# The last column phase of a two-layer scan network: its first finished quarter is handled in two halves of 16 columns

## The chip, the cores and the metric

One core of one Trainium2 chip runs the whole program in one launch. The metric is the device time of an execution, in microseconds (us). The kernel before takes 4107.3 us (median of 3 runs, 4107.22 to 4108.03). One more execution was taken by the profiler; it took 4108.49 us, and every row of the profile is from that one. Engines: PE is TensorE (PEld its weight loads), DVE VectorE, ACT ScalarE, POOL GpSimd, SP SyncE; a row that ends in "q" (SPq, ACTq) is the engine's part in issuing transfers.

## The reference

The input x has 32 images, 48 channels, 64 rows and 128 columns, in float32. Two layers follow one another. Each normalises its input in 16 groups of channels, runs four scans one after the other over the normalised planes, and adds its own input back at the end. The scans go down the rows, up the rows, right over the columns and left over the columns. One step of a scan adds to a line a one-dimensional convolution (48 to 48 channels, 5 taps) of the line before:

```python
def step(w, b):
    def f(carry, inp):
        nxt = inp + _conv1d(carry, w, b)
        return (nxt, nxt)
    return f
```

Each step needs the result of the step before, so a scan over 128 columns is a chain of 127 steps. The left scan begins at the last column and ends at column 0. A column of the result is known as soon as the left scan has passed it; the layer's input at that column is then added (the residual), and the sum is written out in the layout of x.

## The kernel before

The program goes through 12 phases, each a down and up scan over rows or a right and left scan over columns, for a part of the images. The change is in the last one, number 11: the column scans of layer 1 for the second pair of image groups.

**How a column phase is laid out.** The 128 columns are four quarters of 32, quarter 0 at the left edge and quarter 3 at the right. A quarter is six units (`UNITS`, L804: three blocks of channels and lines by two halves of the images); a unit is 128 partitions by 2048 floats, 1 MB. A phase has only three slots of SBUF for its four quarters, so quarter 3 shares a slot with quarter 0: when the right scan has passed quarter 0, `spill_unit` (L823) writes that one to DRAM, `load_unit` (L809) brings quarter 3, and in the left scan, once quarter 3 is finished, `spill_unit` brings quarter 0 back. The scan steps are written in `step` (L902): nine matrix products on PE and three additions on DVE (L929).

**How a quarter is finished.** `load_residual` (L832) brings the layer's input of a unit from the DRAM tensors named `mid` into one of six tiles: four of `arena` and two spare ones, whose rows read `early` (the second spare lies over the weights of the right scan). When the left scan has passed the quarter, `add_residual` (L847, one instruction at L850 on POOL) adds the tile into the unit; `permute_unit` (L865, L872) copies the unit into the tile in the order of the output, 8 copies shared by POOL and ACT; `store_result` (L880) writes the tile to `out` by three or four transfers on the queues of SP and ACT. A store runs along 32 columns, so its packets are 128 B each, 8192 to a unit. Quarter 3 is finished first, then 2, 1 and 0. The last one, quarter 0, is finished after the scan by `last_results` (L1195), where DVE adds and DVE, POOL and ACT copy.

**What else is around.** The phase before leaves some of its results in a DRAM buffer, `held`. During phase 11 SP sends them from there to `out` (`let_result`, L893; rows `out<-held`).

**What sets the order.** `plan_cols` (L1116) writes an agenda: `at(t, fn, ...)` puts a piece of work at a time t that is counted in scan steps, and the program is emitted in that order. `left` is the step at which the left scan begins and `first` of a quarter is `left + 34 + 32 * n_done`, with 4.5 steps between units. Each engine then works through its own list in order, as soon as what a row waits for is there, whatever its time in the agenda. Transfers of the queues of SP and ACT are given eight completion semaphores (`DMAHW0` to `DMAHW7` in the rows below), one after the other, in the order of the builder's schedule and whichever queue they are in; a transfer is issued only when the one that had its semaphore before has landed. One copy on ACT of a single column (L307, `early<-arena 128x1`) reads a column that the left scan writes, at `left + 10`; in the kernel before it stands ahead of the six residual loads of quarter 3, which `plan_cols` puts at `left + 16`, and holds them until that column is there.

Of the kernel before, what the change touches and what calls it, by code (L numbers as in the profile page):

```python
# [31 lines left out]
ALU = mybir.AluOpType  # L32
# [10 lines left out]
E8 = 8  # L43
# [34 lines left out]
def weight_runs():  # L78
# [24 lines left out]
PHASES = (  # L103
    ("rows", 0, 0),
    ("rows", 0, 1),
    ("rows", 0, 2),
    ("rows", 0, 3),
    ("cols", 0, 0),
    ("cols", 0, 1),
    ("rows", 1, 0),  # L110
    ("rows", 1, 1),
# [10 lines left out]
def kernel(  # L122
# [8 lines left out]
    nc = tc.nc  # L131
    B, _, H, W = x.shape
    NK = W // E8
    NH = H // E8
    KQ = NK // NQ
    WQ = W // NQ
    N = NK * GB
    RUN = KQ * GB
# [158 lines left out]
    def dma(dst, src, queue=None):  # L297
        (queue or nc.sync).dma_start(dst, src)
# [21 lines left out]
    def pieces(o):  # L320
        return [(e, c0, c1, p0) for e, c0, c1, g, p0 in PIECES if g == o]
# [3 lines left out]
    def slots(k):  # L325

        return (0, 1, 2) if k % 2 == 0 else (2, 1, 0)
# [476 lines left out]
    UNITS = [(g, half) for g in range(NG) for half in range(2)]  # L804

    def quarter(k, j):
        return slot[slots(k)[j % 3]].rearrange("p (o s n) -> p s o n", s=2, o=NG)
# [50 lines left out]
    def by_image(t):  # L858

        return t.rearrange("p (a e k b) -> p a b k e", a=NH, e=E8, b=GB)  # L860
# [13 lines left out]
    def in_output(j, g, e):  # L874


        t = out[g * GB : (g + 1) * GB].rearrange("b c (a e) w -> e (c a) b w", e=E8)
        return t[e, :, :, j * WQ : (j + 1) * WQ]

    def store_result(k, j, i, perm):  # L880
        pair = PHASES[k][2]
        o, half = UNITS[i]
        for n, (e, c0, c1, p0) in enumerate(pieces(o)):
# [2 lines left out]
            queue = nc.scalar if n % 2 and k == len(PHASES) - 1 else nc.sync  # L886
            dma(dst.rearrange("(c a) b n -> c a b n", a=NH), src, queue)

    def hold_result(j, i, perm):
        o, half = UNITS[i]  # L890
        dma(held[j, half][o], perm, nc.scalar)
# [145 lines left out]
    def at(t, fn, *args):  # L1037
        agenda.append((t, len(agenda), fn, args))

    def spread(t, gen, every):  # L1040


        def go(t):
            if next(gen, "end") != "end":
                at(t + every, go, t + every)
                agenda.sort(key=lambda a: a[:2])

        at(t, go, t)
# [67 lines left out]
    def plan_cols(k, t0, prev):  # L1116
        _, layer, pair = PHASES[k]
        n = 2 * NG
        after = prev == "cols"
        for i in range(n):  # L1120
            early = 30 if after else 58 if k - 1 in JOINED else 54
            at(t0 - early + 2 * i, load_unit, k, 0, i)
            at(t0 + (3 if after else -24 + 2 * i), load_unit, k, 1, i)
            at(t0 + (38 if after else 8) + 2 * i, load_unit, k, 2, i)
            at(t0 + 33 + 2 * i, spill_unit, k, i, False)
            at(t0 + 50 + 2 * i, load_unit, k, 3, i)
        final = k == len(PHASES) - 1
        left = t0 + W - 1
        end = left + W - 1
        for i in range(n):  # L1130

            t = left + 64 + 2 * i if layer == 0 else left + 39.5 + 4.5 * i
            at(t, spill_unit, k, i, True)
        units = []
        for n_done, j in enumerate((3, 2, 1, 0)):
            first, every = left + 34 + 32 * n_done, 4.5
            if j == 0 and PHASES[k + 1 if not final else k][0] == "rows":
                first, every = (end + 29, 6) if pair else (first, 7)
            units += [(first + every * i, j, i) for i in range(n)]
        stats = None  # L1140
        if layer == 0:
            stats = ResultStatsV(f"r{2 * pair}"), ResultStatsA(f"r{2 * pair + 1}")
        tiles = [stage[:, i] for i in range(4)]
        if layer:
            tiles += spare_tiles[0 : 2 if final else 1]
        n = len(tiles)
        direct = [u for u in units if not (final and u[1] == 0)]

        for u, (t, j, i) in enumerate(direct):
            nat = tiles[u % n]  # L1150
            o, half = UNITS[i]
            if u < n:
                at(left + 16, load_residual, k, j, i, nat)
            if layer == 0:
                if u >= n:
                    at(max(direct[u - n][0] + 3, t - 21), load_residual, k, j, i, nat)
                at(t, add_residual, k, j, i, nat)
                at(t + 4, keep_result, k, j, i)
                unit = quarter(k, j)[:, half, o]
                if half == 0:  # L1160
                    for b in range(GB):
                        at(t + 5 + b, stats[0].take, j, o, unit, b)
                else:
                    at(t + 1, stats[1].take, j, o, unit)
            else:

                at(t, add_residual, k, j, i, nat)
                at(t + 2.5, permute_unit, k, j, i, nat, (nc.gpsimd, nc.scalar, nc.scalar))
                if final or j not in HELD:
                    at(t + 4.5, store_result, k, j, i, nat)  # L1170
                else:
                    at(t + 4.5, hold_result, j, i, nat)
                if final and j == 1:
                    at(t + 4.7, load_residual, k, 0, i, last_tiles(k)[i])

                if u >= 2 and u - 2 + n < len(direct):
                    at(t + 4.6, load_residual, k, *direct[u - 2 + n][1:], tiles[(u - 2) % n])
        if layer == 0:
            spread(units[-1][0] + 14, pair_scaling(pair, stats, 8), 1)
        if layer:  # L1180

            at(left + 10, nc.scalar.copy, junk[:, BN - 1 :], quarter(k, 3)[:, 0, 0, RUN - 1 : RUN])
        if layer and not final:
            todo = [(j, half, e) for j in HELD for half in range(2) for e in range(E8)]
            for n, what in enumerate(todo):
                at(end + 63 + 1.9 * n, let_result, *what)
        if final:
            at(end + 4, last_results, k)

    def last_tiles(k):  # L1190

        s = slot[slots(k)[2]].rearrange("p (i n) -> p i n", i=2 * NG)
        return [s[:, i] for i in range(2 * NG)]
# [11 lines left out]
    for k, (kind, *_) in enumerate(PHASES):  # L1205
        n = (H if kind == "rows" else W) - 1
        starts.append(end - 2 * n if k in JOINED else end)
        end = starts[-1] + (2 if k in JOINED else 1) * n + (2 if k + 1 in JOINED else 1) * n
    for k, (kind, layer, _) in enumerate(PHASES):
        (plan_rows if kind == "rows" else plan_cols)(k, starts[k], PHASES[k - 1][0])  # L1210
# [279 lines left out]
```

## Time and profile before

| | before |
|---|---|
| median of 3 runs | 4107.3 us |
| profiled execution | 4108.49 us |
| its span on the core | 4106.8 us |
| PE busy, of the span | 4012.3 us, 98% |
| DVE busy | 2078.8 us, 51% |
| ACT busy | 1306.9 us, 32% |
| POOL busy | 789.0 us, 19% |
| packets of transfers, all | 2253898, of them under 512 B 2008848 |

The span is what the engines and queues record; 1.7 us of the profiled execution lie around it. In the page's 40 slices each digit is a slice of 102.7 us, so the whole left scan of the last phase is in the last three, and slices are too coarse for it: the table by stretches and the lists of transfers with their times are what to read there.

### The profile page before, as it was taken

How to read it: one execution, taken by the hardware profiler on the slowest of the kernel's cores; microseconds unless marked ns; L12 is line 12 of the kernel's file. 1: busy time of each engine (PE TensorE's matmuls, PEld its weight loads, DVE VectorE, ACT ScalarE, POOL GpSimd, SP SyncE). 2: the span in 40 equal slices, each digit the busy share in tenths (PEclk: the TensorE clock that was granted, in tenths of full speed). 3: DMA queues.
4: the chain of work that ended last, by engine and by line, in shares of the span. 5: the costliest groups of instructions: out<-in, count | busy, mean ns of one | idle time of the engine just before them, and what ended most of it. 6: DMA issues, size and time to landing. Idle time of an engine off the chain costs nothing. (4 is left out here: it accounts for less than half of the span.)

```text
span 4106.8 us, 85201 instructions
## 1 busy us (share of the span) xinstructions
PE 4012.3 (98%) x34360; PEld 3927.0 (96%) x34360; DVE 2078.8 (51%) x6137; ACT 1306.9 (32%) x2628; POOL 789.0 (19%) x672
## 2 busy tenths in 40 slices
PE   6999999999999999999999999999999999999994
PEld 5999999999999999999999998888999999999994
DVE  6454454544444567546655443333444444444444
ACT  4557466430000355003773633434000002300122
POOL 5631303100000243002411000000000025610353
PEclk9999999999999999999999999999999999999997
DMA  9898897967993499804996965666698039999799
GB/s 299 220 223 185 245 189 218 171 108 97 147 181 60 141 245 288 193 2 155 242 161 143 142 102 96 101 108 104 103 166 202 1 77 245 299 251 155 147 234 196
DMA packets 2253898, 681.57 MB, mean 166 GB/s; under 512 B 2008848, under 2 KB 2206656, under 8 KB 2231232
## 3 DMA queue, kind: packets, MB, share of 16 engines
q1 hardware_dynamic: 2117568, 595.36, 70.3%
q10 hardware_dynamic: 135936, 80.77, 8.2%
q8 instruction: 270, 4.42, 0.5%
q14 instruction: 124, 1.02, 0.1%
HBM read 399.11 MB, written 295.93 MB: 169 GB/s over the span
## 5 line engine op out<-in xcount | busy, mean ns | idle before, releaser
L850 POOL TENSOR_TENSOR arena<-arena 128x2048 f32<-128x2048 f32 x80 | 362.5, 4547 | 1714.3 <-PE step_00l L915 521.3
L790 ACT ACTIVATE arena<-arena,offsetr,scaler 128x128 f32<-128x128 f32 (+1 forms) x576 | 345.2, 688 | 348.8 <-DMA arena<-mid 322.5
L648 ACT ACTIVATE early<-arena 128x256 f32<-128x256 f32 x192 | 129.7, 676 | 837.0 <-POOL arena L850 830.6
L790 ACT ACTIVATE arena<-arena,offset,scale 128x256 f32<-128x256 f32 (+2 forms) x360 | 249.0, 787 | 91.8 <-DMA arena<-xin 81.6
L709 POOL COPY arena<-arena 128x256 f32<-128x256 f32 x340 | 201.0, 653 | 383.7 <-DMA arena<-in_x 230.2
L915 PE MATMUL step_01r<-arena,early 128*128 128x128 f32 x2286 | 249.8, 272 | 0.0
L915 PE MATMUL step_11r<-arena,early 128*128 128x128 f32 x2286 | 249.2, 272 | 0.0
L915 PEld LDWEIGHTS step_11r<-arena,early 128*128 128x128 f32 x2286 | 248.7, 184 | 0.4 <-DVE arena L929 0.3
L915 PEld LDWEIGHTS step_01r<-arena,early 128*128 128x128 f32 x2286 | 248.9, 184 | 0.2
L915 PE MATMUL step_00r<-arena,early 128*128 128x128 f32 x2286 | 248.8, 272 | 0.0
L915 PEld LDWEIGHTS step_00r<-arena,early 128*128 128x128 f32 x2286 | 248.5, 184 | 0.2 <-DVE arena L929 0.2
L915 PE MATMUL step_10l<-arena,wleft 128*128 128x128 f32 x2286 | 248.5, 272 | 0.0
L915 PE MATMUL step_11l<-arena,wleft 128*128 128x128 f32 x2286 | 248.5, 272 | 0.0
L915 PE MATMUL step_00l<-arena,wleft 128*128 128x128 f32 x2286 | 248.4, 272 | 0.0
L915 PE MATMUL step_01l<-arena,wleft 128*128 128x128 f32 x2286 | 248.4, 272 | 0.0
L915 PE MATMUL step_10r<-arena,early 128*128 128x128 f32 x2286 | 248.4, 272 | 0.0
L915 PEld LDWEIGHTS step_10l<-arena,wleft 128*128 128x128 f32 x2286 | 248.4, 184 | 0.0
L915 PEld LDWEIGHTS step_11l<-arena,wleft 128*128 128x128 f32 x2286 | 248.4, 184 | 0.0
L915 PEld LDWEIGHTS step_00l<-arena,wleft 128*128 128x128 f32 x2286 | 248.4, 184 | 0.0
L915 PEld LDWEIGHTS step_01l<-arena,wleft 128*128 128x128 f32 x2286 | 248.4, 184 | 0.0
L915 PEld LDWEIGHTS step_10r<-arena,early 128*128 128x128 f32 x2286 | 248.4, 184 | 0.0
L872 ACT COPY arena<-arena 128x256 f32<-128x256 f32 x172 | 99.6, 656 | 366.6 <-POOL arena L850 234.7
(545 smaller groups left out, 6870.1 us busy)
## 6 DMA issues: line engine op xcount, KB each, us to landing
xin<-arena SPq DMA_DIRECT2D x94, 512.0 KB, 4.5
arena<-in_x SPq DMA_DIRECT2D x18, 2048.0 KB, 10.5
upa<-arena SPq DMA_DIRECT2D x192, 192.0 KB, 3.8
arena<-upa SPq DMA_DIRECT2D x96, 384.0 KB, 9.9
arena<-xin SPq DMA_DIRECT2D x96, 384.0 KB, 10.6
upb<-arena SPq DMA_DIRECT2D x192, 192.0 KB, 3.9
arena<-upb SPq DMA_DIRECT2D x96, 384.0 KB, 10.9
arena<-xin SPq DMA_DIRECT2D x174, 192.0 KB, 4.2
```

Of the source, the lines that this page charges most:

```text
L648: nc.scalar.activation(junk[:, 0:n], view[:, b], AF.Identity, accum_out=self.sum[:, i, j : j + 1])
L709: copy(dst[:, r, q], src[:, r0 + r, q])
L790: nc.scalar.activation(args[0], args[0], AF.Identity, bias=args[2], scale=args[1])
L850: eng.tensor_tensor(unit, unit, nat, ALU.add)
L872: copy(by_w(perm)[:, a], src[:, a])
L915: nc.tensor.matmul(part(turn(whole(ps[o]))[0:m], -s), weights[:, i, at : at + m], part(turn(src(i)), s), start=seen[o] == 1, stop=seen[o] ...
```

## The change

Quarter 3 of the last phase, the one that is finished first, is handled in two halves of 16 columns: the right half (columns 112 to 127) from 17 steps after the left scan's begin, the left half (96 to 111) at the place where the whole unit was handled. For each half POOL adds the half unit into the residual tile (L900 of the new kernel; the sum stands in the tile, where it stood in the unit before), POOL and ACT copy it back into the unit in the order of the output (L906), and the store takes it from the unit. A store of a half runs along 16 columns, 64 B to a packet, so a half has as many packets as a whole unit had. The six residual loads of quarter 3 are put at `left - 14` to `left - 6` (five) and `left + 2` (the one whose tile lies over the weights), and the six of quarter 2 all follow their unit's stores.

```diff
--- before.py
+++ after.py
@@ -886,6 +886,33 @@
             queue = nc.scalar if n % 2 and k == len(PHASES) - 1 else nc.sync
             dma(dst.rearrange("(c a) b n -> c a b n", a=NH), src, queue)
 
+    def part_of_unit(t, half):
+
+        n = RUN // 2
+        return t.rearrange("p (m h n) -> p h m n", h=2, n=n)[:, half]
+
+    def finish_part(k, j, i, nat, half, store):
+
+        o, g = UNITS[i]
+        unit = quarter(k, j)[:, g, o]
+        here, sums = part_of_unit(unit, half), part_of_unit(nat, half)
+        if not store:
+            nc.gpsimd.tensor_tensor(sums, here, sums, ALU.add)
+            src = by_image(nat)[:, :, :, 2 * half : 2 * half + 2]
+            dst = here.rearrange("p (a b) (k e) -> p a b k e", a=NH, e=E8)
+            for a in range(NH):
+                eng = (nc.gpsimd, nc.scalar, nc.scalar)[a % 3]
+                copy = eng.copy if eng is nc.scalar else eng.tensor_copy
+                copy(dst[:, a], src[:, a])
+            return
+        pair = PHASES[k][2]
+        w0 = half * WQ // 2
+        for n, (e, c0, c1, p0) in enumerate(pieces(o)):
+            dst = in_output(j, 2 * pair + g, e)[c0 * NH : c1 * NH, :, w0 : w0 + WQ // 2]
+            queue = nc.scalar if n % 2 else nc.sync
+            src = here[p0 : p0 + c1 - c0].rearrange("p (a b) n -> p a b n", a=NH)
+            dma(dst.rearrange("(c a) b n -> c a b n", a=NH), src, queue)
+
     def hold_result(j, i, perm):
         o, half = UNITS[i]
         dma(held[j, half][o], perm, nc.scalar)
@@ -1149,6 +1176,13 @@
         for u, (t, j, i) in enumerate(direct):
             nat = tiles[u % n]
             o, half = UNITS[i]
+            if u < n and final:
+                at(left - 14 + 2 * i if i < n - 1 else left + 2, load_residual, k, j, i, nat)
+                for part, first in ((1, left + 17 + 2.5 * i), (0, t - 1)):
+                    at(first, finish_part, k, j, i, nat, part, False)
+                    at(first + 3, finish_part, k, j, i, nat, part, True)
+                at(t + 3, load_residual, k, *direct[u + n][1:], nat)
+                continue
             if u < n:
                 at(left + 16, load_residual, k, j, i, nat)
             if layer == 0:
@@ -1173,7 +1207,7 @@
                 if final and j == 1:
                     at(t + 4.7, load_residual, k, 0, i, last_tiles(k)[i])
 
-                if u >= 2 and u - 2 + n < len(direct):
+                if u >= (n + 2 if final else 2) and u - 2 + n < len(direct):
                     at(t + 4.6, load_residual, k, *direct[u - 2 + n][1:], tiles[(u - 2) % n])
         if layer == 0:
             spread(units[-1][0] + 14, pair_scaling(pair, stats, 8), 1)
```

The order of instructions moves in three places. The first is ACT's list at the end of phase 10's results (`held_111<-arena`) and the begin of the last left scan. `mid_86` and `mid_87` are the residuals of quarter 3; the last two rows of the loads (`early<-mid_87`) are the tile over the weights. Before:

```order
L298 DMA held_111<-arena 128x2048 [waits DMAHW3_49,Activation_49,Pool_49]
L307 COPY early<-arena 128x1 [waits DMAHW5_49,DMAHW6_49,DMAHW4_49,DVE_49]
L298 DMA arena<-mid_86 128x8x256 [waits DMAHW4_49,DMAHW0_49]
L298 DMA arena<-mid_87 128x8x256 [waits DMAHW5_49]
L298 DMA arena<-mid_86 128x8x256 [waits DMAHW6_49,DMAHW1_49]
L298 DMA arena<-mid_87 128x8x256 [waits DMAHW7_49,DMAHW3_49]
L298 DMA early<-mid_86 96x8x256 [waits DMAHW0_49]
L298 DMA early<-mid_86 32x8x256 [waits DMAHW1_49]
L298 DMA early<-mid_87 96x8x256 [waits DMAHW2_49,PE_49]
L298 DMA early<-mid_87 32x8x256 [waits DMAHW3_49]
```

And now:

```order
L298 DMA held_111<-arena 128x2048 [waits DMAHW3_49,Activation_49,Pool_49]
L298 DMA arena<-mid_86 128x8x256 [waits DMAHW5_49,DMAHW0_49]
L298 DMA arena<-mid_87 128x8x256 [waits DMAHW7_49,DMAHW6_49]
L298 DMA arena<-mid_86 128x8x256 [waits DMAHW1_49]
L298 DMA arena<-mid_87 128x8x256 [waits DMAHW3_49]
L298 DMA early<-mid_86 96x8x256 [waits DMAHW5_49]
L298 DMA early<-mid_86 32x8x256 [waits DMAHW7_49]
L298 DMA early<-mid_87 96x8x256 [waits DMAHW6_49,PE_49]
L298 DMA early<-mid_87 32x8x256 [waits DMAHW7_49]
L307 COPY early<-arena 128x1 [waits DMAHW3_49,DMAHW4_49,DMAHW2_49,DVE_49]
```

The eight loads stand ahead of the copy L307 instead of behind it, directly behind the last transfer to `held`, and the first six have no wait but those for semaphores (5 and 0, 7 and 6, 1, 3, 5, 7). Behind L307 come the copies of half units, 128x8x16.

The second place is SP's list in the right scan: the loads of quarters 2 and 3 of phase 11 (`arena<-upb`) and the writes of quarter 0 to DRAM (`spill`). Before:

```order
L298 DMA spill_105<-arena 128x2048 [waits DMAHW0_49]
L298 DMA arena<-upb_95 48x2048 [waits DMAHW1_49,Activation_49,Pool_49]
L298 DMA arena<-upb_95 48x2048 [waits DMAHW2_49]
L298 DMA arena<-upb_95 32x2048 [waits DMAHW3_49]
L298 DMA spill_105<-arena 128x2048 [waits DMAHW4_49]
L298 DMA arena<-upb_94 16x2048 [waits DMAHW5_49,Activation_49,Pool_49]
L298 DMA arena<-upb_94 48x2048 [waits DMAHW6_49]
L298 DMA arena<-upb_94 48x2048 [waits DMAHW7_49]
L298 DMA arena<-upb_94 16x2048 [waits DMAHW0_49]
L298 DMA spill_105<-arena 128x2048 [waits DMAHW1_49]
```

And now:

```order
L298 DMA spill_105<-arena 128x2048 [waits DMAHW4_49]
L298 DMA arena<-upb_95 48x2048 [waits DMAHW6_49,Activation_49,Pool_49]
L298 DMA arena<-upb_95 48x2048 [waits DMAHW0_49]
L298 DMA arena<-upb_95 32x2048 [waits DMAHW1_49]
L298 DMA spill_105<-arena 128x2048 [waits DMAHW2_49]
L298 DMA arena<-upb_94 16x2048 [waits DMAHW3_49,Activation_49,Pool_49]
L298 DMA arena<-upb_94 48x2048 [waits DMAHW4_49]
L298 DMA arena<-upb_94 48x2048 [waits DMAHW5_49]
L298 DMA arena<-upb_94 16x2048 [waits DMAHW6_49]
L298 DMA spill_105<-arena 128x2048 [waits DMAHW7_49]
```

The rows are the same ones; their semaphores are not. Four of them (the `upb_95` row of 32x2048, the first `upb_94` row of 16x2048, the second of 48x2048, and the last `spill`) now have semaphores 1, 3, 5 and 7, which the third to sixth of the residual loads on ACT had just before them.

The third is SP's list where quarter 3 is stored and quarter 0 comes back (`arena<-spill`). Before:

```order
L298 DMA out<-held_111 384x8x32 [waits DMAHW2_49]
L298 DMA out<-held_111 384x8x32 [waits DMAHW3_49]
L298 DMA out<-arena 384x8x32 [waits DMAHW4_49,DMAHW5_49,Activation_49,Pool_49]
L298 DMA out<-arena 256x8x32 [waits DMAHW6_49]
L298 DMA arena<-spill_105 128x2048 [waits DMAHW0_49,DVE_49,PE_49]
L298 DMA out<-arena 384x8x32 [waits DMAHW1_49,Activation_49,Pool_49]
L298 DMA out<-arena 256x8x32 [waits DMAHW3_49]
L298 DMA arena<-spill_105 128x2048 [waits DMAHW5_49]
```

And now, at the stores of the left halves:

```order
L298 DMA out<-arena 384x8x16 [waits DVE_49,DMAHW3_49,Activation_49,Pool_49]
L298 DMA out<-arena 256x8x16 [waits DMAHW5_49]
L298 DMA arena<-spill_105 128x2048 [waits DMAHW5_49,DMAHW7_49,DMAHW3_49,PE_49]
L298 DMA out<-arena 384x8x16 [waits DMAHW1_49,Activation_49,Pool_49]
L298 DMA out<-arena 256x8x16
L298 DMA arena<-spill_105 128x2048 [waits DMAHW3_49,DMAHW6_49,DMAHW2_49,DMAHW1_49]
L298 DMA out<-arena 128x8x16 [waits DVE_49,DMAHW0_49,Activation_49,Pool_49]
L298 DMA out<-arena 384x8x16
L298 DMA arena<-spill_105 128x2048 [waits DMAHW4_49,DMAHW1_49,DMAHW0_49]
```

A reload of quarter 0 had one transfer's semaphore in its row; now there are three or four, among them those of the stores directly ahead of it, which read the unit that the reload writes over.

## The prediction

> **What bounds the kernel now.** I read the page's first two parts, then a table by stretches for the last phase, then the lists of transfers and instructions there.
>
> ```profile
> span 4106.8 us, 85201 instructions
> PE 4012.3 (98%) x34360; PEld 3927.0 (96%) x34360; DVE 2078.8 (51%) x6137; ACT 1306.9 (32%) x2628; POOL 789.0 (19%) x672
> PEclk9999999999999999999999999999999999999997
> ```
>
> PE is the bound for as long as there are scan steps, at the full clock. What happens beside it costs nothing unless it makes a step wait or moves the end. The page's chain of waits holds only `ACT early L872 0%`, so the end has to be taken apart by stretches (columns: us, busy time and instructions of PE, PEld, DVE, ACT, POOL, then the granted clock, the DMA engines' mean share, GB/s):
>
> ```profile
> 3843.00:3871.00 28.00, 28.00 (x260) 28.00 (x259) 13.49 (x43) 2.37 (x5) 6.87 (x5) 1.00 0.01 1
> 3872.00:3931.00 59.00, 59.00 (x546) 59.00 (x545) 29.17 (x91) 14.47 (x25) 34.43 (x21) 1.00 1.24 256
> 3931.00:3996.00 65.00, 65.00 (x601) 65.00 (x600) 31.77 (x100) 19.62 (x35) 40.30 (x29) 1.00 1.18 209
> 3996.00:4050.00 54.00, 53.95 (x497) 53.76 (x495) 26.66 (x84) 12.21 (x22) 31.20 (x20) 1.00 1.28 227
> 4050.00:4107.00 57.00, 0.00 (x0) 0.00 (x0) 25.12 (x19) 13.31 (x23) 12.73 (x18) 0.52 1.30 170
> ```
>
> PE ends at 4050, and the program 57 us later. The DMA engines do nothing from 3843 to 3871 (share 0.01) and are full (1.18 and more) from 3872 to the end. So the tail is a queue of transfers, and the change puts stores of quarter 3 into the idle stretch. What that is worth depends on whether the queue of the early stages reaches the end. These rows (start, length; of a group of issues the time from first to last) mark the stages:
>
> ```profile
> 3864.07 4.54 POOL L850 TENSOR_TENSOR arena<-arena 128x2048 f32<-128x2048 f32 x1 [250.00 <-PE step_11l L915]
> 3871.61 4.01 SPq L298 DMA_DIRECT2D out<-arena  x2
> 3989.18 4.54 POOL L850 TENSOR_TENSOR arena<-arena 128x2048 f32<-128x2048 f32 x1 [24.26 <-DMA arena<-mid]
> 3996.73 30.73 SPq L298 DMA_DIRECT2D out<-arena  x6
> 4050.26 2.28 DVE L850 TENSOR_TENSOR arena<-arena 128x2048 f32<-128x2048 f32 x1
> ```
>
> Quarter 3 is stored from 3871.6, quarter 1 from 3996.7. That second moment is set by the scan: quarter 1's first addition is at 3989.2, some 2 us after the left scan passes that quarter (every quarter is 32 steps, 62.5 us: 3864.1, 3926.6, 3989.1).
>
> **Prices of transfers.** All from stretches in which the 16 DMA engines did little else:
>
> ```profile
> DMA packets 32535, 4.14 MB, mean 165 GB/s; under 512 B 32535, under 2 KB 32535, under 8 KB 32535
> ...
> GB/s 365 352 361 344 381 328 340 352 340 356 348 348 348 352 344 348 352 340 356 348 344 356 344 348 352 348 336 229 217 213 205 242 213 213 172 168 205 176 164 188
> DMA packets 2985, 3.01 MB, mean 301 GB/s; under 512 B 53, under 2 KB 2984, under 8 KB 2984
> ...
> DMA packets 95542, 12.26 MB, mean 153 GB/s; under 512 B 95535, under 2 KB 95535, under 8 KB 95535
> ```
>
> The first is 4075 to 4100, stores of 128-B packets alone: 25 us x 16 / 32535 = 12.3 ns for a packet on an engine; a unit is 8192 packets, 6.29 us. The second is 3822 to 3832, residual loads of 1-KB packets: 10 x 16 / 2985 = 54 ns, 1024 to a unit, 3.4 us (47 ns and 3.0 us at the 350 GB/s of its first two thirds, before the loads run out). The third is 3720 to 3800, `held` to `out`: 80 x 16 / 95542 = 13.4 ns.
>
> **Why filling the gap can pay little.** From 3996.7 on, six units of quarter 1 and six of quarter 0 must be stored, 12 x 6.29 = 75.5 us, and eight residual units loaded (quarter 0's six, and quarter 1's last two, whose tiles come free only in this stage), 8 x 3.1 = 25 us. Together 100.5 us, so the last landing can't come before about 4097. This is quarter 0's and quarter 1's own work; what was stored before can't shorten it. The stretch really moved
>
> ```profile
> DMA packets 110016, 21.94 MB, mean 198 GB/s; under 512 B 101216, under 2 KB 110009, under 8 KB 110009
> ```
>
> (3996 to 4107): 101216 / 8192 = 12.4 units of stores and (21.94 - 12.96) / 1.05 = 8.6 units of loads. Beyond the 12 and the 8 that is 0.4 x 6.29 + 0.6 x 3.1 = 4.4 us of earlier work; the other 4 us to the end near 4106 are not full. Part of the 4.4 is in flight at any such border; I put what the change could take away at 1.5 us, 4 at most.
>
> **What is brought forward.** The DMA work from the first store of quarter 3 to the first store of quarter 1 is six stored units of quarter 3 (37.7), six reloads of quarter 0 (1.05 MB at 350 GB/s, 3.0 each) and six residual units of quarter 2 (3.1 each), 36.6, six stored units of quarter 2 (37.7) and four residual units of quarter 1 (12.4): 124.4 us, from 3871.6 to 3996. It just fits, as the full rows say. Now the first store can come when POOL and ACT have made the half unit after column 112: 16 steps of 62.5 / 32 = 1.95 us earlier than the 3864.1 of now, and a half needs some 5 us less for addition and copies, so from about 3835.5, 36 us earlier. Four terms stand against this.
>
> First, **the packets of 64 B**. A half unit has 8192 of them, so quarter 3 needs 98304 instead of 49152, 6144 on each engine; each ns of their price is 6.1 us. No row has any. From below: were only bytes paid, 6.1 ns, nothing added; from above: a packet of 64 B costs what one of 128 B does, 12.3 ns, 37.7 us added. The line through 12.3 ns at 128 B and 47 to 54 ns at 1 KB gives 9.3 to 9.8 ns; I take 9.6, because both of its rows are of this kernel's own transfers: 59 us for quarter 3, 21.3 us added.
>
> The Trainium skill ("DMA: Bandwidth & Descriptors", section "Why small descriptors are slow (HBM only)") counts 32-B beats and about 3 more cycles for each packet, so 5 cycles against 7. By that ratio the 64-B packet is 12.3 x 5/7 = 8.8 ns, an estimate from that page; quarter 3 would be 54 us and 16 us added, 5 less than by the line, and the rival of the dear packet, below, would be out. No row here shows it.
>
> Second, four of the `held` transfers (two of 384 KB, one of 256, one of 128: 9216 packets of 128 B) now stand between the stores of the right halves on SP: 9216 / 16 x 13.4 ns = 7.7 us.
>
> Third, SP waits before each reload of quarter 0 for the landing of stores that it has only just issued.
>
> ```profile
> L298 SPq DMA_DIRECT2D arena<-spill x6: 1592/4226/8192, 3875.7 to 3933.5; - x6
> DMA to landing us min/median/max: 7.0/11.5/16.1
> ```
>
> Six such waits let the queues run dry by 0 to 1.5 us each; I take half, 5 us. No scan step waits for it: the last reload lands between 3940 and 3950 now, and quarter 0 is needed when the scan has passed quarter 1, near 3988.
>
> Fourth, ACT and POOL get twice as many, half as large instructions. They have idle time in every row of the table (POOL 40 of 65 us, ACT 20 of 65); an addition of half a unit is 2.3 us by elements and 4.54 at most, a half unit's transfers 4.9, so this hides behind the stores. Without that cover it would be 12 x 2.3 = 27 us of POOL's time before quarter 2.
>
> The sum: 124.4 + 21.3 + 7.7 + 5 = 158.4 us from 3835.5, that is 3993.9, 2 us earlier than now. So the early stages finish about as they did, and the end moves by 0 to -1.5 us. I take -0.5.
>
> **The early loads.** They were held by the gate on ACT:
>
> ```profile
> 3615.17 0.35 ACTq L298 DMA_DIRECT2D held<-arena  x1
> 3814.81 0.19 ACT L307 COPY early<-arena 128x1 f32<-128x1 f32 x1 [199.72 <-DVE arena L929]
> 3814.87 6.39 ACTq L298 DMA_DIRECT2D arena<-mid  x4
> ```
>
> Without it nothing stands between them and the last `held` store at 3615.2, and they are issued there, 160 us before the place `left - 14` that their line names. At that moment the right scan is short of its own data:
>
> ```profile
> 3620.00:3640.00 20.00, 20.00 (x187) 20.00 (x186) 9.61 (x30) 0.00 (x0) 0.00 (x0) 1.00 1.02 301
> 3640.00:3664.00 24.00, 24.00 (x223) 24.00 (x223) 11.93 (x38) 0.00 (x0) 0.00 (x0) 1.00 1.02 233
> L298 SPq DMA_DIRECT2D arena<-upb x20: 302/303/1227, 3615.2 to 3651.6; - x20
> DMA to landing us min/median/max: 11.1/12.9/16.2
> 3677.44 1.10 DVE L929 SCALAR_TENSOR_TENSOR arena<-step_11r,bd,arena 128x128 f32<-128x128 f32 x3 [0.87 <-DMA arena<-upb]
> ```
>
> The DMA engines are full, the last load of quarter 2 is issued at 3651.6 and lands 12.9 later, 3664.5; the step of column 64 reads it at 3677.4. The slack is 13 us. Five residual units, 5.24 MB, now go first, because SP's rows there have the semaphores 1, 3, 5 and 7 behind them: at 301 to 350 GB/s they take 15 to 17.4 us, at 233 GB/s 22.5. PE waits for 2 to 9.5 us, or not at all if the loads share better; I take 16 us, a wait of 3. Every later stage hangs on the scan, so this goes to the end undiminished. The sixth load waits for the end of the right scan and is behind nothing that counts. What stands behind the loads on ACT is the gate and the copies of half units, all after 3832.
>
> The sum: 4108.5 + 3 - 0.5 = 4111.0 against the profiled execution, which is 1.2 above the median of the runs; as a median 4110.
>
> **The rivals.** 0.2% of this kernel, 8.2 us, is about what a measurement tells from no change: faster means under 4099.1, slower over 4115.5.
>
> *The 64-B packet costs as much as one of 128 B.* Against the sum, 12.3 - 9.6 = 2.7 ns x 6144 = 16.6 us more, so the early stages end at 4010 instead of 3996, 14 late; that is carried to the end, since the tail is full throughout. With the wait of 3 us: 4108.5 + 14.4 + 3 = 4126, 4125 as a median. It decides from the 2 us of room, about 10 ns, and tells as slower from about 11. For it: the 1-KB rows leave fixed work in every packet (a line through zero would put 128 B at 6 ns, the row has 12.3). Against: there the line still falls. Chance 0.25.
>
> *The early loads hide.* In another stretch, 3500 to 3600, both kinds were in flight:
>
> ```profile
> arena<-upb SPq DMA_DIRECT2D x17, 384.0 KB, 8.8
> arena<-mid ACTq DMA_DIRECT2D x4, 1024.0 KB, 20.0
> ```
>
> The large packets of SP's loads passed the small ones of ACT's (8.8 us to landing against 20.0). If SP keeps its share, quarter 2 is late by less than its 13 us and no step waits: 4107 as a median, 4103 with the 4 us of the stretch after 3996. Against it the semaphores, which make SP wait for ACT's landings. Chance 0.22.
>
> The Trainium skill has the same on the page named above, section "Queues, rings and completion order": each DMA engine goes round its queues packet by packet, so a queue of large packets gets more bytes. The two rows agree with it.
>
> *The gap is worth what it looks like.* If the units of quarter 1 and 0 were late for other reasons than their own transfers, and the early stages' end decided, 10 us could come off: the addition, copies and stores after the scan need 4050.3 + 5 + 6 x 6.29 = 4093, and the other two quarters' overlap leaves about 4098. Against it, the sum of 100.5 us. Chance 0.05.
>
> **How the numbers follow.** The forecast has 0.45, with 4104 to 4115 as its own range; the rivals 0.25, 0.22 and 0.05; 0.03 is left. Likeliest 4110. No difference: 0.45 + 0.22, less a little of each that falls out, 0.65; slower 0.28 (the packets, and a wait over 8 us); faster 0.07. Range 4103 (the hidden loads, with the cleared stretch) to 4125 (the packets).
>
> **What would show it.** Right: the stretch 3843 to 3871 full of 64-B packets near 9.6 ns; an idle time of PE before column 64 of the right scan, ended by a load from `upb`; the first addition of quarter 1 later by just that time; the last stores as before. Wrong: no such wait; 64-B packets at 12 ns, with quarter 1's stores late; or a first store of quarter 1 on time and an end before 4100, which would mean that my 100.5 us are not a bound.

## The result

The changed kernel takes 4137.6 us (median of 4 runs, 4135.9 to 4140.0) against 4107.7 us: a ratio of 1.0073, 95% interval 1.0056 to 1.0091. It is 30 us slower, almost 13 above the end of the predicted range. The profiled execution took 4140.0 us.

The table by stretches of the new kernel (columns as before), with borders at what changed. The DMA share adds up the packets of both queues, so it can exceed 1:

```profile
3676.00:3686.00 10.00, 2.25 (x21) 2.06 (x20) 1.22 (x4) 0.00 (x0) 0.00 (x0) 0.75 1.01 210
3686.00:3693.00 7.00, 7.00 (x42) 7.00 (x43) 2.03 (x7) 0.00 (x0) 0.00 (x0) 0.62 1.02 221
3693.00:3700.00 7.00, 7.00 (x67) 7.00 (x66) 3.50 (x11) 0.00 (x0) 0.00 (x0) 1.00 1.01 229
...
3844.00:3862.00 18.00, 18.00 (x168) 18.00 (x168) 9.04 (x29) 7.58 (x23) 17.39 (x21) 1.00 1.38 92
...
3884.00:3914.00 30.00, 30.00 (x279) 30.00 (x278) 14.77 (x46) 5.11 (x15) 8.68 (x12) 1.00 1.36 163
3914.00:3996.00 82.00, 82.00 (x758) 82.00 (x757) 40.38 (x126) 15.05 (x30) 37.95 (x24) 1.00 1.00 181
...
4007.00:4060.00 53.00, 53.00 (x489) 52.90 (x488) 26.05 (x82) 11.58 (x20) 29.63 (x17) 1.00 1.27 222
4060.00:4138.00 78.00, 0.30 (x3) 0.10 (x1) 23.65 (x20) 18.91 (x33) 20.91 (x22) 0.52 1.25 182
```

Three things stand in it. PE is idle near 3680 and then slow: 42 products in the 7 us from 3686, at a clock of 0.62, where 67 is normal. The stretch that was idle is full of stores, as meant. And from 3914 to 3996, where the stores should have been packed closest, the DMA engines' share is 1.00 instead of some 1.3, although there was more to move than before. The scan ends at 4060 instead of 4050, and the program 78 us after it instead of 57: of 31.5 us between the two profiled spans, 10 are in the scan and 21 in the tail.

The row for the scan, in DVE's timeline of the new kernel:

```profile
3685.41 0.61 DVE L956 SCALAR_TENSOR_TENSOR arena<-step_11r,bd,arena 128x128 f32<-128x128 f32 x2 [7.91 <-DMA arena<-upb]
```

The step of column 64 waited 7.9 us for a load of quarter 2. SP's table of waits (who waited, for what: us in all, times, longest) for 3612 to 3664, where quarter 2 is loaded:

```profile
SPq L298 <- DMA arena<-mid: 19.1, 2, 16.1
SPq L298 <- DMA early<-mid: 8.6, 2, 8.0
```

SP stood 27.7 us before its loads because residual loads of ACT's queue, the users of its semaphores before, had not landed. These were issued at the place that the prediction names, in ACT's timeline:

```profile
3614.04 0.33 ACTq L298 DMA_DIRECT2D held<-arena  x1
3614.46 27.51 ACTq L298 DMA_DIRECT2D arena<-mid  x4
```

The row for the tail, in SP's waits of the new kernel from 3880 to 3996:

```profile
SPq L298 <- DMA out<-arena: 46.2, 7, 10.5
```

SP stood 46.2 us, in seven waits, for stores to land: these are the waits before the reloads of quarter 0. In the kernel before such waits were 2.0 us in 3870 to 3996:

```profile
SPq L298 <- DMA out<-arena: 2.0, 2, 1.6
```

Last, the price of a packet, from all transfers of the new kernel in 3862 to 3866, where nothing but 64-B packets was moved:

```profile
DMA packets 5387, 0.34 MB, mean 86 GB/s; under 512 B 5387, under 2 KB 5387, under 8 KB 5387
```

A packet of 64 B takes 4 us x 16 / 5387 = 11.9 ns; one of 128 B took 12.3. A longer stretch, 3850 to 3860 of the version "The held transfers first" below, has 13660 packets of 64 B in 10 us, 11.7 ns.

So there is a theory A, of three terms that add up: 10 us from the early loads (8 of waiting, 2 of a lower clock), some 15 from SP's waits between stores and reloads, and some 7 from the four `held` transfers and the right halves, which do not fit the idle stretch. Its rivals: B, the tail is a queue of transfers that swallows a late scan, so the terms don't add; C, the tail grew because quarter 3's packets doubled at an unchanged price.

### The profile page after: what moved, and what is told of

Its sections match the earlier page's. It is cut to its first block, busy times and chain, and to the rows that moved or that the text cites. A ratio compares the mean times of both kernels' runs of the same rounds, so it can differ in the third digit from the quotient of the medians.

```text
span 4138.3 us, 85285 instructions
## 1 busy us (share of the span) xinstructions
PE 4015.6 (97%) x34360; PEld 3930.1 (95%) x34360; DVE 2077.9 (50%) x6137; ACT 1310.2 (32%) x2658; POOL 799.0 (19%) x696
## 5 line engine op out<-in xcount | busy, mean ns | idle before, releaser
L850 POOL TENSOR_TENSOR arena<-arena 128x2048 f32<-128x2048 f32 x76 | 344.3, 4549 | 1496.7 <-PE step_00l L942 519.0
L307 ACT COPY early<-arena 128x1 f32<-128x1 f32 x2 | 0.4, 191 | 655.7 <-DVE arena L956 655.7
## 6 DMA issues: line engine op xcount, KB each, us to landing
arena<-upb SPq DMA_DIRECT2D x96, 384.0 KB, 10.1
```

The lines of the kernel that those rows point to most:

```text
L307: fn(*args)
L850: eng.tensor_tensor(unit, unit, nat, ALU.add)
```

## The experiments

**The early loads alone.** The kernel before, with one edit:

```diff
-            if u < n:
+            if u < n and final:
+                at(left - 14 + 2 * i if i < n - 1 else left + 2, load_residual, k, j, i, nat)
+            elif u < n:
                 at(left + 16, load_residual, k, j, i, nat)
```

> The kernel before with one part of the change alone: the residual loads of quarter 3 ahead of the left scan, quarter 3 finished in whole units. Theory A (the loads take turns with the right scan's own loads; the step of column 64 waits 8 us, PE then runs some 2 us at a lower clock, and the 10 us go to the end undiminished): 4107.7 + 10 = 4117.7 us. Rival B (the tail is a queue of transfers, which absorbs a late scan): 4108 to 4111.

Measured: 4120.3 us (4115.9 to 4124.5) against 4107.7, a ratio of 1.0030, interval 1.0019 to 1.0041: 12.6 us slower. DVE's timeline of this kernel has the same wait:

```profile
3687.22 0.61 DVE L929 SCALAR_TENSOR_TENSOR arena<-step_11r,bd,arena 128x128 f32<-128x128 f32 x2 [9.36 <-DMA arena<-upb]
```

9.4 us of waiting, and DVE's first addition after the scan at 4060.9 instead of 4050.3, 10.6 later; the spans of the two profiled executions differ by 10.7. A late scan is not absorbed; B falls.

**The halves without the early loads.** The change, with the loads back behind the copy L307:

```diff
-                at(left - 14 + 2 * i if i < n - 1 else left + 2, load_residual, k, j, i, nat)
+                at(left + 16, load_residual, k, j, i, nat)
```

> The change with its residual loads of quarter 3 put back behind the copy that waits for column 119 or so of the left scan (left + 16, as before); halves as in the change. Theory A: no step waits in the right scan, 4137.6 - 10 = 4127.6. Rival B: the queue of transfers sets the end, and the loads now stand where the right halves are stored: 4134 to 4140.

Measured: 4130.5 us (4128.4 to 4130.8), 7.1 below the change, and no wait at column 64. Nearer to A's 10 than to nothing. The 3 us that are missing aren't settled: the ranges of the two, four executions each, leave 5 to 12, and here the residual loads share the stretch after 3815 with the right halves' begin.

**The reloads of quarter 0 later.** The change, with one number:

```diff
-            t = left + 64 + 2 * i if layer == 0 else left + 39.5 + 4.5 * i
+            t = left + 64 + 2 * i if layer == 0 else left + (53 if final else 39.5) + 4.5 * i
```

> The change with one number altered: the six reloads of quarter 0 are put 13.5 steps (three units) later, so that SP no longer waits, between the stores of the left halves, for the landing of stores that it has just issued. Theory A (these waits leave the DMA engines part idle from 3914 to 3996, where their share is 0.86 to 1.12 against 1.2 to 1.4 around, about 15 us of work; that is most of the 21 us that the tail grew): 4137.6 - 12 to 15 = 4123 to 4126. Rival C (the tail grew because quarter 3 has twice the packets at almost the same price each, 11.9 ns against 12.3): nothing gained, 4135 to 4138.

Measured: 4123.8 us (4120.9 to 4127.9), 13.9 below the change, with every packet still there. The table by stretches of this kernel:

```profile
3914.00:3996.00 82.00, 82.00 (x758) 82.00 (x757) 40.24 (x127) 17.92 (x35) 37.94 (x24) 1.00 1.25 217
```

And SP's waits in it, for 3880 to 3996:

```profile
SPq L298 <- PE step_11l L942: 9.7, 2, 5.9
SPq L298 <- POOL arena L900: 4.5, 1, 4.5
SPq L298 <- POOL arena L906: 2.9, 1, 2.9
```

The waits for landings of stores are gone from the table, the share is 1.25, and 217 GB/s are moved instead of 181: over 82 us, 82 x 36 / 217 = 13.6 us' worth of transfers, about the gain. The waits were the largest term of the tail. As the one cause of its growth, C falls.

**Both edits.** Loads at `left + 16` and reloads 13.5 steps later.

> The change with both edits: residual loads at left + 16, reloads of quarter 0 three units later. Theory A, terms that add up: 4137.6 - 10 - 12 to 15 = 4113 to 4116. Rival C (packets): 4126 to 4128. Rival B: 4134 to 4140.

Measured: 4116.2 us (4113.4 to 4117.5), ratio to the kernel before 1.0018, interval 1.0009 to 1.0027. The two gains add: 7.1 + 13.9 = 21.0 against 21.4 measured. 8.5 us are left.

**The held transfers first.** To the version with both edits:

```diff
-                at(end + 63 + 1.9 * n, let_result, *what)
+                at(end + 63 + 1.6 * n, let_result, *what)
```

> The version with both edits (residual loads at left + 16, reloads of quarter 0 three units later; 4116.2 us), and the transfers from held to out 1.6 steps apart instead of 1.9, so that the last four stand ahead of the stores of the right halves on SP. Theory A (the 8.5 us that are left over the kernel before come from the four transfers, 7.7 us, which wait behind the first right half while the DMA engines have room): 4109 to 4111. Rival D (they come from the right halves' own packets, 36 us at 11.9 ns, which end after the place where the left halves begin, whatever the order): 4115 to 4117.

Measured: 4109.4 us (4106.0 to 4111.3), ratio 1.0000, interval 0.9990 to 1.0009. (This version and the three that follow ran on another chip than the four above, beside the kernel before at 4108.1 us.) The last four `held` transfers had stood behind the first right half while the DMA engines had room; with both edits they were issued from 3839.9 on, here SP has sent them before 3809:

```profile
3689.47 119.49 SPq L298 DMA_DIRECT2D out<-held  x58
3838.00 75.03 SPq L298 DMA_DIRECT2D out<-arena  x20
```

The time is 6.8 us less (8.5 above the kernel before there, 1.3 here), and nothing is left that the interval, some 4 us to either side, would show. All three terms of A are now taken away one by one, and with quarter 3 still stored in halves of 64-B packets the kernel is as fast as the one before. D, that the right halves' packets cost something in themselves, falls.

**No stores of the right halves.** The version with both edits:

```diff
-                    at(first + 3, finish_part, k, j, i, nat, part, True)
+                    if part == 0:
+                        at(first + 3, finish_part, k, j, i, nat, part, True)
```

> The version with both edits, without the stores of the right halves: columns 112 to 127 of these images are not written. Half of quarter 3's 98304 packets are gone. Theory A (the right halves fill a stretch that was idle, and only their overflow of some 7 us counts): 4107 to 4110. If the doubled packets as a whole counted, 36 us of them: 4090 or less.

Measured: 4108.8 us (4106.8 to 4112.2), ratio 1.0000, interval 0.9991 to 1.0009. 36 us of the DMA engines' work are left out, and the end stands where it stands in the kernel before. So does the first store of quarter 1 on SP, at 3996.7 in both.

**Whole stores from the unit.** The version with both edits, sums and copies in halves, one store of a whole unit:

```diff
+    def store_whole(k, j, i):
+        o, half = UNITS[i]
+        store_result(k, j, i, quarter(k, j)[:, half, o])
...
-                    at(first + 3, finish_part, k, j, i, nat, part, True)
+                    if part == 0:
+                        at(first + 3, store_whole, k, j, i)
```

> The version with both edits, where sums and copies are made in halves as in the change, but each unit is stored once, whole, from the unit, when its left half is done: 8192 packets of 128 B instead of twice 8192 of 64 B, and nothing is stored in the idle stretch. Theory A (a packet of 64 B costs what one of 128 B does, so the left halves' stores alone take as long as whole units): the same time as without the right halves' stores, within 2 us, and 4107 to 4110. If 64-B packets were cheaper (9.6 ns), this one is longer by 8 us than that without the right halves' stores.

Measured: 4107.1 us (4106.0 to 4108.7), ratio 0.9997, interval 0.9988 to 1.0007. It moves twice the bytes that the run above moves in these stores, in as many packets, and is not longer. It doesn't tell the price of a packet apart, though: the run above shows that even without 36 us of work the end stays. The price rests on the row of 3862 to 3866 and the longer stretch beside it.

**Early loads behind column 72.** The change with later reloads, `held` at 1.6 steps, and its loads behind one more copy on ACT:

```diff
+        if final:
+            at(t0 + 73, nc.scalar.copy, junk[:, BN - 1 :], quarter(k, 2)[:, 0, 0, 15:16])
```

> The change with the reloads three units later, the held transfers 1.6 steps apart, and its early residual loads behind a copy on ACT that reads column 72 of quarter 2, which the right scan writes at about 3693 us: the loads are still ahead of the left scan, but behind the loads that column 64 waits for. Theory A (the stall came from the order of the loads alone): no wait at column 64, 4107 to 4111, like the version with loads at left + 16. Rival (early loads cost wherever they stand in the right scan, since the DMA engines are full there): 4115 to 4120.

Measured: 4120.7 us (4116.2 to 4123.4), ratio 1.0029, interval 1.0020 to 1.0039. No step waits at column 64, as A said, yet the time is the rival's. The rows are of the fastest of its executions, 4116.2 us; there the scan ends on time, and the first store of quarter 1 is at 4007.1, 10.4 late. SP's timeline in this kernel:

```profile
3718.28 131.50 SPq L298 DMA_DIRECT2D out<-held  x60
3849.95 72.50 SPq L298 DMA_DIRECT2D out<-arena  x20
```

SP's waits, 3690 to 3850:

```profile
SPq L298 <- DMA arena<-mid: 26.7, 2, 23.4
SPq L298 <- DMA early<-mid: 6.8, 2, 5.8
```

And the table by stretches:

```profile
3690.00:3705.00 15.00, 15.00 (x141) 15.00 (x140) 7.32 (x24) 0.19 (x1) 0.00 (x0) 1.00 0.76 237
```

SP again stood 33.5 us before semaphores of residual loads, the DMA engines' share fell to 0.76 meanwhile, `held` ended some 40 us later than in the version above with loads at `left + 16`, and the right halves began at 3850 instead of 3838. There the loads run from 3815, when SP has nothing more to send before column 112 is through, and cost nothing. So the loads' earlier place has a price of its own beside the wait at column 64; how the 11 us between these two versions divide between the late start and what follows from it was not taken apart.

## Why the prediction was wrong

**What failed.** The prediction named the mechanisms, and mis-sized three terms of its sum: the packets of 64 B (21.3 us added; 35.4 by the measured price), SP's waits before the reloads (5 us; 13.9) and the wait of the scan (3 us; 10.1). With the measured terms the sum closes: 124.4 + 35.4 + 7.7 + 13.9 = 181.4 us from 3835.5, that is 4016.9, 20.9 late, and with the scan's 10.1 it is 31.0 us, against 31.5 between the two profiled executions. Of the prediction's own signs, the first addition of quarter 1 came later by just the scan's delay (3999.2), and the sign of being wrong came too, packets near 12 ns with quarter 1's stores late. The first of these on SP in the new kernel, in the kernel before at 3996.73:

```profile
4026.02 40.15 SPq L298 DMA_DIRECT2D out<-arena  x8
```

**The bound: right as the way to the end, not tested as a limit.** From the first store of quarter 1 on SP to the end of the span are 110.1 us in the kernel before, 112.3 in the new one and 107.3 to 110.2 in the eight other versions, whether that store was on time or 29 us late. So what makes that store late is what is paid. No version stored quarter 1 earlier than 3996.7, since the scan has not passed it before; so whether the 100.5 us are a least, or the rival of "The gap is worth what it looks like" has something in it, stays open. "Filling the gap can pay little" came true, and the runs show a nearer reason, below: the left halves alone are the old work. Also right: that ACT issues the early loads directly behind the last `held` store, that SP hangs on them by the semaphores, which step of the scan waits, and that its 10 us reach the end undiminished.

**"I take 16 us, a wait of 3": mis-sized; 10.** The term of 16 us was the residual units' bytes at the rate of a stretch in which one queue had the engines. The last load of quarter 2 that column 64 waits for landed near 3685 instead of 3664.5: 20.5 us late, less 13 of slack, is the wait of 7.9. The row at 233 GB/s, which gave 22.5 and was kept as the upper end, was the nearer one. The new kernel moved 265 GB/s there, at which 5.24 MB take 19.8 us:

```profile
3620.00:3682.00 62.00, 58.07 (x535) 57.88 (x533) 28.23 (x88) 0.00 (x0) 0.00 (x0) 0.99 1.03 265
```

The share stayed at 1.03 while SP stood for 27.7 us. Whether the loads would have shared the engines better without the waits for semaphores is not shown; no version alters the semaphores alone. The other 2 us were missing from the sum. After the idle time PE did 42 products in 7 us instead of 67, at a clock of 0.62 in the row, which is 2.6 us by those counts; the scan's end gives 10.1 - 7.9 = 2.2.

The Trainium skill ("TensorE: Matmul & The Clock Gate", section "Part 1: The HAM clock gate (the "warmup" mystery)") says that the clock is halved after an idle window of about 3.4 us and comes back after as much work. The trace agrees as far as its rows go: 7.9 us idle, then a clock of 0.62 over 7 us and 1.00 after.

**"I take half, 5 us": mis-sized; 13.9.** The prediction let each of SP's six waits drain the queues by 0 to 1.5 us. What it left out is what stands behind SP while it waits. Six of ten of the left halves' transfers are SP's, and they stand in its list behind the reload, whose row names the store issued a moment before. So SP could have one unit's transfers in flight at a time: a store, then the reload, then the next. The row that the prediction shows there, 7.0 to 16.1 us to landing, is of the reloads, not of the stores that SP waits for; in the new kernel SP's stores of halves took 9.7 to 9.9 us to landing (medians of 3914 to 3980). Six waits of that size are 58 us, against 46.2 measured. What they cost, 13.9 us by the run with later reloads, is less, as ACT's queue still moved: the engines' share in 3914 to 3996 was 1.00, not zero.

**"9.6 ns for a packet of 64 B": wrong; 11.9.** The line through 128 B and 1 KB doesn't hold below 128 B. By the rate, quarter 3's packets cost 6144 x 2.3 ns = 14 us more of DMA time than I summed. That used up the room. With nothing else in the way, 3835.5 + 124.4 + 35.4 = 3995.3, just on time, and so the version with the `held` transfers first is level with the kernel before. But no room was left for the `held` transfers, and none for SP's waits. At 9.6 ns the sum with the measured waits would have ended at 4002.8, 6.8 late instead of 20.9 (an estimate by the sum; no run has cheaper packets). It is also why this change doesn't gain: at an equal price per packet, the left halves (six times 8192 packets) take as long as six whole units did, so storing them alone is the old work. The rival of the dear packet was right about the price and, by this sum, about its being carried to the end; its 4125 lacks the rest of SP's waits and of the wait of the scan.

The count of cycles from the Trainium skill ("DMA: Bandwidth & Descriptors", section "Why small descriptors are slow (HBM only)") gave an estimate of 8.8 ns; the row has 11.9, and the measurement decides.

**"9216 / 16 x 13.4 ns = 7.7 us" for the held transfers: right,** 6.8 to 7.2 measured as the gain of sending them first.

**POOL and ACT at half size: right.** An addition of half a unit takes 2.4 us, as in POOL's timeline of the new kernel, and SP's waits for POOL between 3880 and 3996 are under 10 us in all beside the 46.2 for stores:

```profile
3840.59 2.39 POOL L900 TENSOR_TENSOR arena<-arena 128x1024 f32<-128x1024 f32 x1 [227.66 <-DVE arena L956]
```

**The rival of the hidden loads: wrong.** In the new kernel too ACT's loads took longer from issue to landing than SP's (26.5 us against 12.0, medians of 3615 to 3680), but SP's wait is ahead of the issue, where the size of packets doesn't count. Nor do such landings show that large packets pass small ones: ACT's transfers have 1024 KB and SP's 384, and by the KB ACT's were no slower (39 a us against 32; in the prediction's pair 51 against 44). So the rule of queues served in turn that the Trainium skill states ("DMA: Bandwidth & Descriptors", section "Queues, rings and completion order") is neither borne out nor refuted by these two rows.

**The range.** Its upper end took one loss at a time. With all upper ends in one sum, 9.5 us at column 64, 12.3 ns, and 9 for SP's waits, the early stages end at 3993.9 + 16.6 + 4 = 4014.5, 18.5 late, and the end is 4108.5 + 18.5 + 9.5 = 4136.5, a little over 4135 as a median. The losses add here, as each makes the first store of quarter 1 later.

## What to carry to other kernels

When transfers of two queues share a ring of completion semaphores, a transfer moved ahead on one engine can stop the other engine's list: look up who had each semaphore before, and whether that one can be slow, before calling a prefetch free. A reload into a buffer that is still being stored belongs some units behind that store in the issuing engine's list (three here); directly behind it, the queue holds one unit at a time. And cutting a store in two along its contiguous run doubles its packets; where a packet of half the size costs the same, the second half takes as long as the whole, and an idle stretch filled with the first half is no gain.

## What the runs showed of the hardware

A packet of 64 B took 11.9 ns on a DMA engine where one of 128 B took 12.3: at this size the bytes count for almost nothing (86 GB/s against 165 for the 16 engines). An idle time of 7.9 us on PE cost 2.2 us more in the scan behind it, at a granted clock of 0.62 over 7 us.
